# A graph network on one core: gathered rows come by node, are added in pairs on VectorE, and two one-hot products take the rest

## The chip, the cores and the metric

The kernel runs on one core of a Trainium2 chip. The core has a matrix engine (TensorE, PE in the profile, with its weight loads as PEld), VectorE (DVE), ScalarE (ACT), GpSimd (POOL) and the queue engine SyncE (SP); 16 DMA engines move data. The metric is device time in microseconds of one execution, the median of several runs.

## The reference

There are 6250 nodes with 256 float32 channels and 100,000 edges, sorted by destination. Four layers follow each other; each adds to every node the sum over its incoming edges and puts the result through three dense layers (64 channels in the middle of the last one).

```python
def agg(h):
    return jax.ops.segment_sum(h[src], dst, num_segments=N)
for l in range(NL - 1):                      # NL = 4
    h = x + agg(x)
    h = relu(h @ W1s[l] + b1s[l])
    h = relu(h @ W2s[l] + b2s[l])
    x = h @ W3s[l] + b3s[l]
h = x + agg(x)
h = relu(h @ cW1 + cb1); h = relu(h @ cW2 + cb2)
return h @ cW3 + cb3
# around it: x + ref(relu(layernorm(x)), src, dst, ...)
```

## The kernel before

The nodes form 49 blocks of 128. Since aggregation is linear, W1 is applied before it, and W3 of a layer is merged with W1 of the next. The current rows lie in `XY` in SBUF, as a high and a low half (float32r, 256 columns each), and in a table in HBM. The sums of a destination block are made in one of two ways.

**Panel products (L1470 to L1509).** For most blocks a matrix of edge counts (49 source blocks by 128 destinations, one byte each) is built once, in layer 0. Four blocks make a panel. For each of the 49 source blocks ("units"), a tile of counts is cast to float32r (L1464 on ACT, L1466 on DVE, some units ahead: `prepare`) and four products accumulate (two channel halves, high and low). The loop over layers, panels and units is the backbone of the order: `tick` counts units in `now`.

**Gathered blocks (class `Gathered`, L1264 to L1409).** For the other blocks the source rows are fetched by index: each indirect DMA on GpSimd's queue (L1309) brings 128 rows of 1 KB. The edges are packed in order of destination. Each half block (64 nodes) has 9 tiles of 128 edges, so a block has 18. VectorE makes one-hot matrices of 32 columns (L1334), and PE multiplies them with the rows in four column groups at once (L1353). A block takes two such "visits". Then VectorE adds the block's own row and the sums (L1371, L1380), PE transposes (L1391), and the dense layers follow (`mlp`: L1183, L1212).

In layer 0, 22 blocks are gathered, and 27 stand in seven panels, the first of which has three blocks. In layers 1 to 3, 18 blocks are gathered, and 31 stand in eight panels.

**The building of the matrices (`build`, L1013).** Of a block, 16 steps each make one-hots on VectorE (L994, one of each kind for two steps), multiply them on PE (L1035, two products a step) and cast the result to bytes (L1043 on ACT, L1045 on DVE, by turns). The steps of the first panel run ahead of the first product, all with their cast on ACT (`PRE` units); the others run beside the products of layer 0, by a list of goals.

**Pacing.** A planner's clock adds up the time that PE's work is expected to take (`passed`; the constants stand at L1420). `work_of(l)` is a layer's expected time. `Gathered.begin` spreads a layer's gathers evenly from the layer's start to 10 us before its end. Each row is asked for `LEAD` = 21 us ahead of the visits' schedule, and each gather also waits for the panel product that was last issued when it was asked for (`after`). `gath` has 24 row buffers in layer 0 and 26 later. Jobs such as transposes and dense layers have a first and a last unit, and run at a visit if one falls between.

**Preparation (`look`, L607; `normed`, L819).** The layer norm and the first product with W1 run for all nodes, and beside them the edge windows are found and fetched (`asks`, L601). For the gathered blocks, the tables of source indices (`idx`) and relative destinations (`rel`) are made here (L697 to L731 and L787 to L806). If a check finds that a half block has over 1152 edges, or another bound is passed, a general kernel (`any_edges`) runs afterwards.

Of the kernel before, what the change touches and what calls it, by code (L numbers as in the profile page):

```python
# [8 lines left out]
F32 = mybir.dt.float32  # L9
I32 = mybir.dt.int32  # L10
# [386 lines left out]
def sorted_edges(  # L397
# [56 lines left out]
    Q = P // 4  # L454
    TS = 9
    T = 2 * TS
    CUT = (3, 5)

    ROUNDS = [(3, 3), (4, 4), (0, 5), (1, 6), (2, 7), (None, 8)]
# [10 lines left out]
    gone = [(0, 4), (4, 4), (8, 4), (12, 4), (16, 1), (44, 4), (48, 1)]  # L470
    panels = [(17, 3), (20, 4), (24, 4), (28, 4), (32, 4), (36, 4), (40, 4), (44, 4)]
    S0 = 2 * panels[0][0]
    assert gone[-2] == panels[-1] and sorted(
        b + i for b, n in gone[:-2] + gone[-1:] + panels for i in range(n)) == list(range(NT))
    NQ = len(gone)
    PW = 4 * T

    left = [T * sum(n for _, n in gone[:q]) for q in range(NQ + 1)]

# [7 lines left out]
    clT = const.tile([P, 2, GSUB, NSUB - S0], BF16, name="clT")  # L487
    cT, loT = clT[:, 0], clT[:, 1]
    idx = const.tile([P, left[NQ]], I32, name="idx")
    rel = const.tile([P, left[NQ]], F32, name="rel")  # L490
# [7 lines left out]
    tables = [dram.tile([N, C], F32, name=f"table{l}") for l in range(NLAYER + 1)]  # L498
# [108 lines left out]
    def look(pool):  # L607
# [23 lines left out]
        nc.vector.memset(one, 1.0)  # L631
        firsts = pool.tile([1, EB], F32, name="near", bufs=1)
# [24 lines left out]

        place_i = pool.tile([P, NQ, PW], I32, name="hi", bufs=1)
        for q, (b, _) in enumerate(gone):
            nc.gpsimd.iota(place_i[:, q, :], pattern=[[1, PW]], base=T * b, channel_multiplier=-TS)  # L660
        place = pool.tile([P, 1], F32, name="place", bufs=1)
        nc.gpsimd.iota(place, pattern=[[0, 1]], base=0, channel_multiplier=P,
                       allow_small_or_imprecise_dtypes=True)
        node = pool.tile([P, GSUB], F32, name="node", bufs=1)
# [26 lines left out]
        for q in range(GSUB):  # L691
            for w, e in ((wd, dst), (ws, src)):
# [4 lines left out]
        both = pool.tile([P, 2], F32, name="both", bufs=1)  # L697
        sel = pool.tile([P, NQ, PW], F32, name="near_i", bufs=1)
        some = pool.tile([P, NQ, PW], F32, name="rel", bufs=1)
        nc.vector.tensor_copy(both[:NSUB, 0:1], first[:NSUB, 0:1])  # L700
        nc.vector.tensor_copy(both[:NSUB, 1:2], low[:NSUB])
        nc.vector.tensor_scalar(some[:NSUB], place_i[:NSUB], float(TS - 1), None, op0=OP.is_le)
        nc.vector.scalar_tensor_tensor(sel[:NSUB], place_i[:NSUB], 0.0, some[:NSUB],
                                       op0=OP.is_ge, op1=OP.mult)
        ps = ps_m.tile([P, W], F32, name="ps")
        for q in range(NQ):
            nc.tensor.matmul(ps[:PW, 2 * q:2 * q + 2], sel[:NSUB, q, :], both[:NSUB, :],
                             start=True, stop=True)
        spread = pool.tile([P, NQ, 2], F32, name="spread", bufs=1)
        nc.vector.tensor_copy(spread[:PW], ps[:PW, :2 * NQ].rearrange("p (q t) -> p q t", t=2))  # L710

        part = pool.tile([P, NQ], F32, name="part", bufs=1)
        nc.vector.scalar_tensor_tensor(part[:PW], spread[:PW, :, 1], float(-T), spread[:PW, :, 0],
                                       op0=OP.mult, op1=OP.add)
        for q, (b, _) in enumerate(gone):
            nc.vector.tensor_scalar(part[:PW, q:q + 1], part[:PW, q:q + 1], place[:PW, 0:1],
                                    float(T * P * b), op0=OP.add, op1=OP.add)
        skip = pool.tile([P, NQ], F32, name="skip", bufs=1)  # L720
        nc.vector.tensor_scalar(skip[:PW], part[:PW], float(E - P), None, op0=OP.min)
        from_i = pool.tile([P, NQ], I32, name="from_i", bufs=1)
        nc.vector.tensor_copy(from_i[:PW], skip[:PW])
        nc.vector.tensor_tensor(skip[:PW], part[:PW], skip[:PW], OP.subtract)
        base = pool.tile([P, NQ], F32, name="base", bufs=1)
        nc.vector.tensor_scalar(base[:PW], spread[:PW, :, 1], -1.0, None, op0=OP.add)
        gds = pool.tile([P, 2, NQ, P], I32, name="near_i", bufs=1)
        gd, gs = gds[:, 0], gds[:, 1]
        for q, (_, n) in enumerate(gone):
            for w, e in ((gd, dst), (gs, src)):  # L730
                asks.append((w[:n * T, q, :], e, from_i[:n * T, q:q + 1]))  # L731
# [3 lines left out]
        H = GSUB // 4  # L735
        for q0 in range(0, GSUB, H):
            cut = slice(q0, q0 + H)
            ask(len(asks) - 2 * (GSUB - q0 - H) - 2 * NQ)
            r = pool.tile([P, H, P], F32, name="rel", bufs=1)
            f = pool.tile([P, H, P], F32, name="f", bufs=1)  # L740
# [183 lines left out]
    with tc.manual_schedule():  # L924
# [163 lines left out]
        def job(first, last, fn):  # L1088

            jobs.append((now[0] + first, now[0] + last, fn))  # L1090

        queue = []

        def step(visit):

# [524 lines left out]
```

## Time and profile before

| | |
|---|---|
| median of 3 runs | 2350.51 us (2348.21 to 2352.5) |
| the profiled execution | 2343.82 us, span 2342.0 us |
| mean granted clock of PE | 0.98 |
| share of the span busy | PE 93%, DVE 42%, ACT 38%, POOL 61% |
| gathers | 1368 (396 in layer 0, 324 in each later layer) |
| panel products | 6076, of which 784 are 384 columns wide and 5292 are 512 wide |
| records of the one-hot products | 3344 (two to each of 1672 products) |
| HBM read and written | 310.61 and 58.07 MB |

Lines such as L1309 are those of the kernel before. A busy time is the time in which at least one instruction of a group ran. Matmuls overlap in their pipeline and their ends are modelled, so the time that one takes from PE is read from start to start, and a busy PE is not one at its peak.

### The profile page before, as it was taken

The numbers are of one execution on the slowest core, as the hardware profiler recorded it, in microseconds if no ns is written. First come the engines' busy times: TensorE is split into PE (matmuls) and PEld (weight loads), VectorE is DVE, ScalarE is ACT, GpSimd is POOL, SyncE is SP. The second block draws the span as 40 slices with busy tenths as digits, with TensorE's granted clock in tenths as the row PEclk, the third lists the DMA queues.
The fourth block names the chain that finished last, engine by engine and source line by source line (L and its number), as shares of the span: only waits on it lengthen the run. The fifth ranks groups of instructions, "written<-read, shape, count | busy, mean of one in ns | idle before, by whom it ended". The sixth has DMA issues, their size and how long they took to land. (4 is left out here: it accounts for less than half of the span.)

```text
span 2342.0 us, 34300 instructions
## 1 busy us (share of the span) xinstructions
PE 2175.8 (93%) x12062; PEld 1570.0 (67%) x12062; DVE 972.8 (42%) x2844; ACT 891.8 (38%) x1816; POOL 1429.4 (61%) x1442
## 2 busy tenths in 40 slices
PE   5888998999998999999999999999999999999898
PEld 3656666666665877676766877777677866666565
DVE  6887656556555422222223422222224423232222
ACT  4775545454545423232223432232233322222221
POOL 3635666666666266666666366666664566666663
PEclk9979999999999999999999999999999999999999
DMA  4545555555556554444455554545445655545553
GB/s 151 152 154 176 173 158 174 159 166 173 164 173 200 165 151 151 149 131 149 148 156 178 181 152 134 170 136 161 140 152 159 182 167 156 168 143 172 158 153 107
DMA packets 195882, 371.43 MB, mean 159 GB/s; under 512 B 32790, under 2 KB 122986, under 8 KB 195700
## 3 DMA queue, kind: packets, MB, share of 16 engines
q0 software_dynamic: 67264, 181.96, 26.9%
q1 hardware_dynamic: 126510, 185.34, 24.2%
q8 instruction: 96, 1.57, 0.3%
q10 hardware_dynamic: 1926, 1.85, 0.3%
q14 instruction: 86, 0.70, 0.1%
HBM read 310.61 MB, written 58.07 MB: 157 GB/s over the span
## 5 line engine op out<-in xcount | busy, mean ns | idle before, releaser
L1309 POOL DMA_INDIRECT rows<-table,idx x1368 | 1374.1, 1004 | 830.7 <-PE agg L1491 276.0
L1491 PE MATMUL agg<-a,XY 128*128 128x512 f32 (+1 forms) x6076 | 1484.3, 394 | 52.6 <-issue 39.0
L1491 PEld LDWEIGHTS agg<-a,XY 128*128 128x128 f32 x6076 | 1108.4, 189 | 334.6 <-issue 126.0
L1464 ACT CAST a<-at 128x512 fp32r<-128x512 uint8 (+1 forms) x943 | 546.9, 607 | 694.7 <-PE agg L1491 528.9
L1466 DVE CAST a<-at 128x512 fp32r<-128x512 uint8 (+1 forms) x576 | 256.2, 459 | 582.2 <-PE agg L1491 397.8
L1353 PE MATMUL sums<-rows,hot 128*32 128x256 f32 x3344 | 240.4, 387 | 8.1 <-issue 4.4
L1043 ACT CAST at<-bp 128x392 uint8<-128x392 f32 x276 | 131.3, 488 | 277.8 <-PE bp L1035 197.4
L1045 DVE CAST at<-bp 128x392 uint8<-128x392 f32 x220 | 124.1, 564 | 218.2 <-PE bp L1035 152.3
L1353 PEld LDWEIGHTS sums<-rows,hot 128*32 128x32 f32 x3344 | 106.0, 110 | 132.1 <-issue 72.2
L1035 PE MATMUL bp<-hi,lo 128*128 128x196 bf16 x992 | 143.7, 264 | 47.3 <-issue 18.7
L1035 PEld LDWEIGHTS <-lo 128*128 128x128 bf16 x992 | 76.0, 102 | 129.4 <-issue 86.6
L1380 DVE TENSOR_TENSOR u<-u,sums 128x256 f32<-128x256 f32 x76 | 31.8, 419 | 309.4 <-PE agg L1491 301.4
L1183 PE MATMUL ps<-h,w 128*128 128x512 f32 (+5 forms) x392 | 158.3, 544 | 0.5 <-issue 0.5
L994 DVE TENSOR_TENSOR hi<-cols,pairs 128x784 bf16<-128x784 bf16 x248 | 139.3, 562 | 0.0
L1212 PE MATMUL ps<-w,h 128*128 128x256 f32 x588 | 134.8, 380 | 3.4 <-PE ps L1212 1.6
L1334 DVE TENSOR_TENSOR hot<-colf,rel 128x64 f32<-128x64 f32 x836 | 126.9, 220 | 0.0
L1212 PEld LDWEIGHTS ps<-w,h 128*128 128x128 f32 x588 | 110.5, 190 | 20.2 <-issue 2.7
L1183 PEld LDWEIGHTS ps<-h,w 128*128 128x128 f32 (+1 forms) x392 | 67.2, 184 | 65.3 <-issue 56.4
L1230 DVE TENSOR_TENSOR zz<-ps,w 128x512 f32<-128x512 f32 (+1 forms) x78 | 50.2, 658 | 137.8 <-PE ps L1212 82.3
L994 DVE TENSOR_TENSOR lo<-lanes,pairs 128x512 bf16<-128x512 bf16 x248 | 104.2, 420 | 2.6 <-ACT pairs L989 1.4
L1186 ACT ACTIVATE h<-ps,bias 128x512 f32<-128x512 f32 (+5 forms) x98 | 60.6, 634 | 114.1 <-PE ps L1183 81.6
L1398 ACT ACTIVATE h<-ps,bias 128x256 f32<-128x256 f32 (+1 forms) x84 | 33.5, 450 | 149.4 <-PE agg L1491 48.8
(138 smaller groups left out, 744.9 us busy)
## 6 DMA issues: line engine op xcount, KB each, us to landing
at<-mat SPq DMA_DIRECT2D x189, 448.0 KB
mat<-at SPq DMA_DIRECT2D x31, 784.0 KB
rows<-table,idx POOLq DMA_INDIRECT x1368
table<-zz SPq DMA_DIRECT2D x69, 256.0 KB
back<-table SPq DMA_DIRECT2D x118, 128.0 KB
at<-mat SPq DMA_DIRECT2D x25, 336.0 KB
xs<-in_x_dram SPq DMA_DIRECT2D x8, 768.0 KB
table<-zs SPq DMA_DIRECT2D x24, 256.0 KB
```

Source lines behind the costliest of these rows:

```text
L994: nc.vector.tensor_tensor(o.rearrange("p q (n t) -> p q n t", t=2), values.rearrange("p (n t) -> p n t", t=2)[:, None, :, :].to_broadcast( ...
L1035: mm = nc.tensor.matmul(bp[:, m * HW:(m + 1) * HW], lo[:, q + m, :], hi[:, q + m, :], start=True, stop=True)
L1043: nc.scalar.copy(o, v)
L1045: nc.vector.tensor_copy(o, v)
L1183: mm = nc.tensor.matmul(ps[:mp, :w], weights[l][0][:, c, i * P:i * P + mp], h1[:, c, :w], start=(c == 0), stop=(c == KC - 1))
L1212: mm = nc.tensor.matmul(o, h2[0][:, c, nodes], w3[:, c, :], start=(c == 0), stop=(c == KC - 1))
L1309: got = nc.gpsimd.indirect_dma_start(out=t, out_offset=None, in_=tables[self.l][:, :], in_offset=bass.IndirectOffsetOnAxis(ap=idx[:, o:o + ...
L1334: nc.vector.tensor_tensor(hot[:, i, :, :], colf[:, None, i * Q:(i + 1) * Q].to_broadcast([P, 2, Q]), rel[:, o + k:o + k + TS + 1:TS, None] ...
L1353: nc.tensor.matmul(self.sums[(2 * h + m) * Q:(2 * h + m + 1) * Q, :C], self.hots[r, m][:, h, :], self.rows[g, h, k], start=(r == 0), stop= ...
L1464: nc.scalar.copy(o, mat[l, p][j])
L1466: nc.vector.tensor_copy(o, mat[l, p][j])
L1491: mm = nc.tensor.matmul(agg[c][:, :w], XY[:, j, o:o + P], a[:, :w], start=(j == 0 and half == 0), stop=(j == NT - 1 and half == 1))
```

## The change

The rows of a gathered block now come by node: gather k (k from 0 to 16) brings, for each of the 128 nodes, the row of its k-th edge. A node with fewer edges gets row N + p, one of 128 rows of zeros that are added to each table. Gathers 0 to 15 land in pairs, in 512-column tiles, and VectorE adds them: seven 128x512 adds. It then folds the two halves, gather 16 and the block's own row together (four 128x256 operations). What a node has beyond 17 edges goes to up to 256 overflow slots of its block, as two more gathers (`over`) and two one-hot products 128x128 by 128x256 on PE. A block thus has 19 gathers, and PE's sums are one visit.

Block 16 moves from the gathered blocks to the first panel, which now has four blocks: 21 blocks are gathered in layer 0 and 17 later, and 28 and 32 stand in panels. `PRE` follows, with 16 more build steps ahead of the first product.

In preparation each node's first edge and number of edges are found by counting (`count`), and the first 17 sources of each node are fetched by 21 indirect DMAs. The index table is finished at build step 50 (`slot_rows`), where layer 0's gathers now begin. The overflow slots of a block are found two blocks ahead (`overflow`: two products with two columns each, three small operations and one 256-wide one on VectorE, two indirect DMAs of one element to a partition). The bound of the check is now 256 overflow edges to a block.

Three in four of the byte casts beside the products now run on ACT (half before). The rows are asked for 13.0 us ahead in layer 0 and 16.5 us later (21 before). There are 7 pair buffers in layer 0 and 10 later, and four single ones; the build's PSUM pool has two buffers (three before), and the second cast ring 8 (9 before).

```diff
-    gone = [(0, 4), (4, 4), (8, 4), (12, 4), (16, 1), (44, 4), (48, 1)]
-    panels = [(17, 3), (20, 4), (24, 4), (28, 4), (32, 4), (36, 4), (40, 4), (44, 4)]
+    K, OV = 17, 2
+    SLOT = K + OV
+    gone = [(0, 4), (4, 4), (8, 4), (12, 4), (44, 4), (48, 1)]
+    panels = [(16, 4), (20, 4), (24, 4), (28, 4), (32, 4), (36, 4), (40, 4), (44, 4)]
...
+        zeros = pool.tile([P, C], F32, name="zeros", bufs=1)
+        for t in tables:
+            nc.gpsimd.dma_start(out=t[N:, :], in_=zeros)
...
+        def count(q0):
+            for t in range(1, GD):
+                nc.vector.tensor_scalar(below[:, t - 1], cT[:, q0:q0 + H, :], float(STEP * t),
+                                        None, op0=OP.is_lt)
...
+        for c in range(NG):
+            asks.append((idx[:, c, :], src, from_i[:, c:c + 1]))
...
+    def slot_rows():
+        nc.vector.scalar_tensor_tensor(live, idx, pad[:, 1:2], live, op0=OP.add, op1=OP.mult)
+        nc.vector.tensor_scalar(idx, live, pad[:, 0:1], None, op0=OP.add)
+
+    def overflow(hots, c):
+        nc.vector.tensor_scalar(hit, slots, gained[:, c:c + 1], None, op0=OP.is_ge)
+        for j in range(OV):
+            nc.tensor.matmul(ps[:, 2 * j:2 * j + 2], hit[:, j * P:(j + 1) * P], taken[:, c, :],
+                             start=True, stop=True)
+        def edges():
+            nc.vector.tensor_copy(rel[:, c, :], v[:, :, 0])
+            nc.vector.scalar_tensor_tensor(e, v[:, :, 1], nodes3[:, 2, c:c + 1], line, op0=OP.add,
+                                           op1=OP.add)
+            nc.vector.tensor_scalar(e_i, e, float(E - 1), None, op0=OP.min)
+        def gather():
+            for j in range(OV):
+                asks.append((over[:, j, c:c + 1], src, e_i[:, j:j + 1]))
+            ask(OV)
...
-                    if step % 2 or step <= 2 * PRE:
+                    if step % 4 != 2 or step <= 2 * PRE:
                         nc.scalar.copy(o, v)
                     else:
                         nc.vector.tensor_copy(o, v)
...
+                for g in range(len(self.blocks)):
+                    behind = 3 if g < len(self.blocks) - 1 else 0
+                    self.events.append((SLOT * g + 8, lambda g=g: self.spots(g), False))
+                    for k in range(3, K - 1, 2):
+                        self.events.append((SLOT * g + k, lambda g=g, k=k: self.pair(g, k), False))
+                    self.events.append((SLOT * g + K - 1, lambda g=g: self.fold(g), False))
+                    self.events.append((SLOT * g + SLOT - 1 + behind, lambda g=g: self.add(g), True))
...
-                for r in rounds:
-                    for h in range(2):
-                        for m, k in enumerate(ROUNDS[r]):
-                            if k is not None:
-                                nc.tensor.matmul(
-                                    self.sums[(2 * h + m) * Q:(2 * h + m + 1) * Q, :C],
-                                    self.hots[r, m][:, h, :], self.rows[g, h, k], start=(r == 0),
...
+            def pair(self, g, k):
+                t = self.rows.pop((g, k))
+                if k == 3:
+                    self.acc = work.tile([P, 2, C], F32, name="acc", bufs=1)
+                    nc.vector.tensor_tensor(self.acc, self.rows.pop((g, 1)), t, OP.add)
+                else:
+                    nc.vector.tensor_tensor(self.acc, self.acc, t, OP.add)
+
+            def spots(self, g):
+                hot = self.hot[g] = work.tile([P, OV, P], F32, name="hot", bufs=2)
+                nc.vector.tensor_tensor(hot, colf[:, None, :].to_broadcast([P, OV, P]),
+                                        rel[:, c, :, None].to_broadcast([P, OV, P]), OP.is_equal)
+
+            def fold(self, g):
...
+                nc.vector.tensor_tensor(u, u, self.acc[:, 0, :], OP.add)
+                nc.vector.tensor_tensor(u, u, self.acc[:, 1, :], OP.add)
+                nc.vector.tensor_tensor(u, u, self.rows.pop((g, K - 1)), OP.add)
+            def add(self, g):
+                for j in range(OV):
+                    mm = nc.tensor.matmul(sums[:, :C], hot[:, j, :], self.rows.pop((g, K + j)),
+                                          start=(j == 0), stop=(j == OV - 1))
...
-        LEAD, TAIL = 21.0, 10.0
+        TAIL = 10.0
+        LEADS, DEEP = (13.0,) + (16.5,) * NLAYER, (7,) + (10,) * NLAYER
...
-        ) as ps_a, tc.tile_pool(name="ps_b", bufs=3, space=PSUM) as ps_b:
+        ) as ps_a, tc.tile_pool(name="ps_b", bufs=2, space=PSUM) as ps_b:
+            READY = 50
+                if built[0] == READY:
+                    slot_rows()
+                    layers[0].begin()
```

More of the change, by code (lines that the diff above doesn't have):

```diff
@@ L705, in look @@
[L705 to L716, printed above, removed]
@@ L1117, in tick @@
                 first, last, fn = task
-                if first <= now[0] and (visit or last <= now[0]):
+                if max(first, held[0]) <= now[0] and (visit or last <= now[0]):
                     jobs.remove(task)
```

337 lines of the change are left out of this document (185 added, 152 removed).

## The prediction

> **What bounds the kernel now.** I read the profile page first, then the busy time of each engine by stage. The stages run from one change in the panel products to the next: preparation, the first panel's matrix, then the four layers.
>
> ```profile
> PE 2175.8 (93%) x12062; PEld 1570.0 (67%) x12062; DVE 972.8 (42%) x2844; ACT 891.8 (38%) x1816; POOL 1429.4 (61%) x1442
> ```
>
> ```profile
> 0.00:127.70 127.70, 91.20 (x418) 68.98 (x418) 95.18 (x257) 75.02 (x160) 55.26 (x74) 0.95 0.48 148
> 127.70:158.20 30.50, 22.77 (x114) 12.07 (x114) 26.77 (x63) 25.40 (x66) 9.20 (x8) 0.55 0.52 163
> 158.20:779.70 621.50, 567.20 (x3537) 389.66 (x3537) 370.87 (x1017) 319.40 (x703) 401.98 (x388) 0.99 0.54 167
> 779.70:1298.20 518.50, 504.14 (x2712) 375.74 (x2713) 159.93 (x504) 165.04 (x314) 320.68 (x324) 1.00 0.51 156
> 1298.20:1813.20 515.00, 502.05 (x2706) 374.87 (x2705) 155.80 (x499) 162.47 (x309) 320.54 (x324) 1.00 0.51 155
> 1813.20:2342.00 528.80, 488.49 (x2581) 348.67 (x2579) 164.26 (x507) 144.48 (x268) 321.71 (x324) 0.97 0.51 156
> ```
>
> The columns after the length are PE, PEld, DVE, ACT and POOL (busy us and count), granted clock, DMA. In layers 1 and 2 PE is busy 97% of the time at full clock and DVE 31%: a microsecond taken from PE there is a microsecond of the run. In layer 0 PE is busy 91%, DVE 60%, ACT 51%. PE hardly ever waits for gathered rows:
>
> ```profile
> PE bp L1035 <- ACT at L1043: 9.3, 12, 1.7
> PE agg L1491 <- ACT h L1507: 8.5, 5, 3.1
> PE bp L1035 <- DVE at L1045: 4.7, 3, 2.2
> PE bp L1035 <- DVE hi L994: 4.3, 7, 1.5
> PE bp L1035 <- DVE lo L994: 2.4, 2, 1.3
> PE sums L1353 <- DMA rows<-table,idx: 2.3, 4, 0.7
> ```
>
> These are PE's waits in layer 0 (us in all, times, longest). POOL looks free at 61%, but its own timeline says otherwise. In the middle of a layer, gathers stand back to back, and 0.30 us passes between two even when nothing is waited for:
>
> ```profile
> 448.95 0.96 POOL L1309 DMA_INDIRECT rows<-table,idx  x1 [0.30 <-issue]
> 450.21 0.95 POOL L1309 DMA_INDIRECT rows<-table,idx  x1 [0.30 <-issue]
> ```
>
> So a gather costs POOL its own time and 0.30 us. In layer 0 that is 401.98/388 = 1.036 + 0.30 = 1.34 us, in layers 1 to 3 about 320.7/324 = 0.990 + 0.30 = 1.29 us. The gathers of layer 0 run from the first of these rows to the second, those of layer 1 from the third to the last:
>
> ```profile
> 159.49 0.95 POOL L1309 DMA_INDIRECT rows<-table,idx  x1 [19.10 <-PE agg L1491]
> ...
> 759.48 0.95 POOL L1309 DMA_INDIRECT rows<-table,idx  x1 [0.30 <-issue]
> 798.93 1.19 POOL L1309 DMA_INDIRECT rows<-table,idx  x1 [38.50 <-ACT a L1464]
> ...
> 1282.22 0.96 POOL L1309 DMA_INDIRECT rows<-table,idx  x1 [0.30 <-issue]
> ```
>
> That is 600/388 = 1.55 us a gather in layer 0 and 483/324 = 1.49 in layer 1: POOL is at 87% of what it can issue in both. PE binds, and POOL is close behind.
>
> **The change part by part.** PE's prices come from its timeline in layer 2 (start, length, count of matmul records). A float32 product is two records; a panel product is one.
>
> ```profile
> 1358.81 2.75 PE L1212 MATMUL ps<-w,h 128*128 128x256 f32 x12
> 1361.49 1.50 PE L1353 MATMUL sums<-rows,hot 128*32 128x256 f32 x24
> 1362.92 10.27 PE L1491 MATMUL agg<-a,XY 128*128 128x512 f32 x44
> ...
> 1310.05 21.85 PE L1491 MATMUL agg<-a,XY 128*128 128x384 f32 x124
> ```
>
> *One-hot products.* A visit takes 1362.92 - 1361.49 = 1.43 us, and there are two to a block. The new two products have the form of the first row: 2.68/12 = 0.223 us a record, four records, 0.89 us a block. The wider first panel: 10.27/44 - 21.85/124 = 0.057 us on each of 196 products, 11.2 us a layer.
>
> Layers 1 to 3, each: -36 x 1.43 + 17 x 0.89 + 11.2 = -25.2 us; one block fewer to transpose gives 0.3 more. Three layers: **-76 us**, all on the path, if POOL and DVE keep up.
>
> Layer 0: -44 x 1.43 + 21 x 0.89 + 11.2 = -33.0 us on PE. The overflow step adds two 2-column products to a block. No row has that form; between 0 and 0.3 us each, I take 0.13, 5 us for the 19 blocks that fall in the layer: -28 us.
>
> *A fourth block ahead of the first product.* 16 more build steps run in the second stage, where PE's granted clock is 0.55:
>
> ```profile
> 140.11 5.42 PE L1035 MATMUL bp<-hi,lo 128*128 128x196 bf16 x24 [0.18 <-ACT at L1043]
> 146.39 1.65 PE L1035 MATMUL bp<-hi,lo 128*128 128x196 bf16 x8 [0.86 <-DVE hi L994]
> 148.22 0.83 PE L1035 MATMUL bp<-hi,lo 128*128 128x196 bf16 x4 [0.18 <-ACT at L1043]
> ```
>
> 32 records, or 16 steps, take 148.22 - 140.11 = 8.1 us: **+8 us**. DVE is nearly full there (26.77 of 30.50), so the two passes that finish the index table and the overflow steps of two blocks come on top, about +3 us. In preparation, four counting passes, the node tables and 21 index fetches take the place of seven blocks' edge tables; DVE's work there is about equal, between 0 and +6 us; I take +2. Four stores of zero rows join POOL's queue in that stage, where POOL is busy 55 of 128 us: nothing.
>
> *VectorE.* Prices (mean ns behind the busy time), as this view groups them:
>
> ```profile
> L994 DVE TENSOR_TENSOR hi<-cols,pairs 128x784 bf16<-128x784 bf16 x248 | 139.3, 562 | 0.0
> L1334 DVE TENSOR_TENSOR hot<-colf,rel 128x64 f32<-128x64 f32 x836 | 126.9, 220 | 0.0
> L1045 DVE CAST at<-bp 128x392 uint8<-128x392 f32 x220 | 124.1, 564 | 218.2 <-PE bp L1035 152.3 <-PE agg L1491 49.9 <-remote 14.9
> ...
> L1371 DVE TENSOR_TENSOR u<-XY 128x256 f32<-128x256 f32 x76 | 31.8, 419 | 0.0
> ...
> L1202 DVE TENSOR_TENSOR xt<-xt,cb3r 128x512 f32<-128x512 f32 x21 | 13.6, 685 | 0.0
> ```
>
> A pair add has the form of L1202, 685 ns; seven to a block. Three more 256-wide adds and a 256-wide one-hot go by L1371, 419 ns. A block gains 7 x 0.685 + 4 x 0.419 = 6.5 us and loses 126.9/76 = 1.7. Layers 1 to 3 gain 17 x 6.5 - 18 x 1.7 = 80 us each on a DVE with 360 us idle: hidden, at nothing. What hides it is the idle time and the five or six panel tiles that are cast ahead; if an add waited for late rows, the casts queued behind it on DVE would be late, and PE after them. Layer 0 gains 99 us, plus some 17 for the overflow step, and loses 110 casts of 564 ns (62 us): about 425 of 621 us. ACT takes those 110 casts: +54 us, 373 of 621. Neither engine is full, but in every second pair both casts now go to ACT and the products have two PSUM buffers, not three. The waits for casts and one-hots quoted above sum to 20.7 us; they may double or, with PE held elsewhere, vanish; I take +4.
>
> *GpSimd.* Layer 0 still has 399 gathers (396 before), and 38 overflow fetches come into it. Such a fetch has this row's form, about 1.07 + 0.30 us:
>
> ```profile
> L601 POOL DMA_INDIRECT ws<-in_src_dram,starts x16 | 17.0, 1060 | 4.9 <-issue 4.9
> ```
>
> And a gather that begins while a two-input SBUF operation runs on DVE takes longer:
>
> ```profile
> 137.66 0.56 DVE L994 TENSOR_TENSOR hi<-cols,pairs 128x784 bf16<-128x784 bf16 x1
> 137.81 1.23 POOL L1309 DMA_INDIRECT rows<-table,idx  x1 [0.30 <-issue]
> ...
> 139.15 0.42 DVE L994 TENSOR_TENSOR lo<-lanes,pairs 128x512 bf16<-128x512 bf16 x1
> 139.34 1.05 POOL L1309 DMA_INDIRECT rows<-table,idx  x1 [0.30 <-issue]
> ```
>
> The first began with 0.41 us of DVE's operation left and lost 0.28 against 0.95; the second with 0.23 left lost 0.10. So the loss is what is left, less 0.13. A pair add of 0.685 us catches a gather's start in 0.55/1.4 = 40% of cases and costs it 0.28 on average: 0.11 us; a 0.419 one costs 0.03. A block of 19 gathers gains (7 x 0.11 + 5 x 0.03)/19 = **0.05 us a gather**. Bounds: 0 if the adds always fall between starts, and 0.36 if every microsecond of these adds (6.9 a block) delayed POOL in full. I take 0.05.
>
> The Trainium skill (SBUF — State Buffer, § Who interferes with whom) says that a DVE instruction with two SBUF inputs contends with a GpSimd instruction that reads SBUF, and that whoever issues first holds the shared pair for the whole instruction. The two rows agree in kind and come 0.13 us cheaper than a full hold; by the rule to the letter layer 0 would lose some 12 us more than by the rows.
>
> POOL in layer 0 then needs 395 x (1.34 + 0.05) + 38 x 1.37 = 601 us after the first product, which starts at 158.2 + 8 + 3 + 2 = 171. (Pacing lets only four of the 399 go earlier; before, eight went.) The last gather goes out at 772; with 3 us to land and some 12 of work behind it the layer ends at 787, and at 791 with the cast waits. By PE alone it would end at 779.7 - 28 + 13 = 765. **POOL ends last in layer 0**: rows come late, DVE waits for them in order, PE waits for DVE. Against 779.7 this is **+11 us**, where PE's list promised -15.
>
> In layers 1 to 3 POOL needs 323 x (1.29 + 0.05) = 433 us. The window shrinks from 483 by 25, and by 5 more as the last row is asked for earlier ahead of its use: 453. At 96% it holds, with a few late rows: **+5 us** for the three.
>
> Sum: -76 + 11 + 5 = **-60 us**. The profiled execution took 2343.8 us (span 2342.0 and 1.8 around it), 6.7 below the median of 2350.5. Forecast 2283.8 for such an execution, **2290 us** as a median; its own range, from the bounds of the gather's delay (0 to 0.09) and the cast waits, 2272 to 2312.
>
> **The rivals.**
>
> *PE binds everywhere.* If the adds fall between gather starts and POOL catches up during PE's long float32 stretches, layer 0 ends near 765: -76 - 15 = -91, **2259 us**. For it: POOL had 13% slack. Against it: the 38 fetches and PE's shorter list use up the slack by themselves. Chance 0.20.
>
> *POOL binds in layers 1 to 3 too.* At 0.10 us a gather the need is 323 x 1.39 = 449 of 453, and any unevenness is lost; layer 0 ends near 811. -76 + 31 + 20 = -25: **2325 us**. Chance 0.15.
>
> *Slower: the adds hold up the gathers.* The price is the delay of a gather, e. Layer 0 grows by 4 us for each 0.01 of e, the later layers by 3.2 each once 323 x (1.29 + e) exceeds 453, at e = 0.11. At e = 0.14 the gain is gone; at 0.20 layer 0 ends at about 850, and each later layer needs 481 + 41 = 522 against about 520. +71 and 3 x 2: **2427 us**. For it: adds run when rows land, that is while POOL issues. Against it: only a start is caught. Chance 0.16.
>
> *It doesn't do what it says.* If a block has over 256 edges beyond 17 a node, the general kernel runs afterwards, at a price far above all of these. The given edges have at most 191. Chance 0.01.
>
> **How the numbers follow.** Forecast 0.44 (2272 to 2312), with 0.04 left for something within 0.2% of 2350.5, about what a measurement here tells from no change. Faster: 0.44 + 0.20 + 0.15 = 0.79; same 0.04; slower 0.17. The range 2250 to 2370 leaves out the far end of the first rival (0.04) and most of the slower cases (0.13).
>
> **What would show it.** Right: the sums' matmuls fall to 288 records; in layers 1 to 3 PE stays at 96% or more and each is about 490 us long; in layer 0 POOL's gathers stand 0.30 us apart nearly throughout, and DVE waits for rows. The mean gather shows e: 1.00 us before, about 1.05 after. Wrong: layer 0 ends by 770 with gaps on POOL (first rival); layers 1 to 3 above 500 us with DVE waiting for rows (the others); PE waiting for casts in layer 0 by over 30 us, which I priced at 4.

## The result, and the profile after

The changed kernel takes **2439.68 us** (median of 4 runs, 2436.01 to 2444.74), the kernel before 2351.51 beside it (4 runs, 2348.21 to 2352.9): ratio 1.0379, interval 1.0356 to 1.0401. It is 3.8% slower; the forecast was 2290 and its range ended at 2370. The profiled execution has a span of 2438.2 us, 96.2 more than before. First the page's line of busy times, then the busy time by stage with the columns of the prediction. The stages are cut at the same events: preparation, the first panel's matrix, four layers.

```profile
PE 2121.0 (87%) x9071; PEld 1576.9 (65%) x9071; DVE 1243.0 (51%) x2785; ACT 960.3 (39%) x1925; POOL 1521.2 (62%) x1495
```

```profile
0.00:131.20 131.20, 91.02 (x445) 70.35 (x445) 92.97 (x258) 74.61 (x155) 47.11 (x68) 0.93 0.47 144
131.20:192.30 61.10, 31.83 (x151) 16.71 (x151) 38.41 (x96) 34.46 (x85) 25.72 (x26) 0.53 0.31 95
192.30:877.70 685.40, 561.82 (x2681) 403.46 (x2681) 419.95 (x969) 370.27 (x809) 452.13 (x433) 0.92 0.50 154
877.70:1394.50 516.80, 484.16 (x1970) 368.15 (x1971) 226.56 (x484) 165.61 (x305) 332.50 (x323) 0.99 0.51 157
1394.50:1910.70 516.20, 480.21 (x1971) 368.27 (x1971) 228.35 (x484) 164.63 (x305) 331.55 (x323) 0.99 0.51 156
1910.70:2438.20 527.50, 471.95 (x1857) 349.98 (x1855) 236.72 (x496) 150.73 (x270) 332.16 (x323) 0.95 0.51 158
```

PE has 55 us less to do, as most of the one-hot products are gone, and yet the run is longer. The first product comes 34 us later (192.3, was 158.2), layer 0 is 64 us longer, and layers 1 to 3, where 25 us each should have gone, are as long as before (518.5, 515.0 and 528.8). In layer 1 PE's busy time fell by 20 us (504.14 to 484.16) and its idle time rose by 18 (14.4 to 32.6).

PE's waits in layer 0, then one line of VectorE's waits there:

```profile
PE bp L1108 <- ACT at L1116: 47.7, 26, 8.4
PE bp L1108 <- issue: 43.5, 30, 4.4
PE bp L1108 <- DVE hi L1067: 7.6, 8, 2.8
PE bp L1108 <- DVE at L1118: 5.5, 5, 1.8
```

```profile
DVE acc L1420 <- DMA rows<-table,idx: 2.4, 1, 2.4
```

PE waits for the byte casts (47.7 us, 9.3 before) and, for another 43.5, for nothing that the profile shows. VectorE hardly waits for rows, and GpSimd needs only 452.13 + 433 x 0.30 = 582 of the 685 us. So the engine that was to end last in layer 0 does not: the forecast's mechanism is not what this profile shows.

**A hand-off in layer 1 shows what does hold engines up here.** This is its timeline: PE transposes two blocks (L1472), and ScalarE then takes them out (L1479). Only the rows of these two engines are shown.

```profile
1036.03 0.62 ACT L1545 CAST a<-at 128x512 fp32r<-128x512 uint8 x1 [0.92 <-PE agg L1572]
1036.13 0.60 PE L1472 MATMUL ps<-ident,u 128*128 128x128 f32 x4
1036.48 5.76 PE L1572 MATMUL agg<-a,XY 128*128 128x512 f32 x24
1043.19 0.84 ACT L1479 ACTIVATE h<-ps,bias 128x256 f32<-128x256 f32 x2 [6.55 <-issue]
1043.92 0.62 ACT L1545 CAST a<-at 128x512 fp32r<-128x512 uint8 x1
1044.59 0.73 PE L1572 MATMUL agg<-a,XY 128*128 128x512 f32 x2 [2.34 <-ACT h L1479]
```

The transposes end at 1036.73 and ScalarE is free from 1036.65, but it starts at 1043.19, 6.5 us later. Its casts stand behind, PE uses up the six tiles that are cast (24 products) and then stands still for 2.3 us. ScalarE waits for PE's semaphore alone there, so the signal reached it late. In the trace's records such signals are updates of semaphores. After one at 1040.31 the next of PE's is recorded at 1046.02, and six stand between 1046.02 and 1046.28: a pause and then a burst. ScalarE's start at 1043.19 has no update of its own on record. PE has 2825 instructions that raise its semaphore, and only 2477 separate updates are recorded (2685 and 2277 in the profile of before). Whether the others arrived together with one of these or are only missing from the records can't be told.

### The profile page after: what moved, and what is told of

It reads as the page before. It is cut to its first block, busy times and chain, and to the rows that moved or that the text cites. A ratio compares the mean times of both kernels' runs of the same rounds, so it can differ in the third digit from the quotient of the medians.

```text
span 2438.2 us, 28824 instructions
## 1 busy us (share of the span) xinstructions
PE 2121.0 (87%) x9071; PEld 1576.9 (65%) x9071; DVE 1243.0 (51%) x2785; ACT 960.3 (39%) x1925; POOL 1521.2 (62%) x1495
## 5 line engine op out<-in xcount | busy, mean ns | idle before, releaser
L1572 PE MATMUL agg<-a,XY 128*128 128x512 f32 x6076 | 1593.2, 412 | 85.1 <-issue 46.0
L1394 POOL DMA_INDIRECT rows<-table,idx x1152 | 1181.8, 1026 | 667.5 <-PE agg L1572 258.8
L1545 ACT CAST a<-at 128x512 fp32r<-128x512 uint8 x943 | 564.4, 622 | 801.1 <-PE agg L1572 527.1
L1547 DVE CAST a<-at 128x512 fp32r<-128x512 uint8 x576 | 256.6, 452 | 598.6 <-PE agg L1572 371.4
L1422 DVE TENSOR_TENSOR acc<-acc,rows 128x512 f32<-128x512 f32 x432 | 295.8, 685 | 2.5 <-DMA rows<-table,idx 0.4
L1394 POOL DMA_INDIRECT last<-table,over x144 | 155.4, 1079 | 58.9 <-issue 28.7
L1260 PE MATMUL ps<-h,w 128*128 128x512 f32 (+2 forms) x364 | 160.4, 576 | 13.9 <-DVE zz L1301 6.8
L1118 DVE CAST at<-bp 128x392 uint8<-128x392 f32 x110 | 62.0, 564 | 115.3 <-PE bp L1108 78.6
L1394 POOL DMA_INDIRECT last<-table,idx x72 | 77.6, 1078 | 30.7 <-issue 14.3
L1461 DVE TENSOR_TENSOR u<-u,sums 128x256 f32<-128x256 f32 x72 | 30.1, 418 | 99.5 <-PE agg L1572 94.7
L1451 PE MATMUL sums<-last,hot 128*128 128x256 f32 x288 | 76.8, 387 | 4.3 <-DMA last<-table,over 3.2
```

The lines of the kernel that those rows point to most:

```text
L1118: nc.vector.tensor_copy(o, v)
L1260: mm = nc.tensor.matmul(ps[:mp, :w], weights[l][0][:, c, i * P:i * P + mp], h1[:, c, :w], start=(c == 0), stop=(c == KC - 1))
L1394: got = nc.gpsimd.indirect_dma_start(out=t, out_offset=None, in_=tables[self.l][:, :], in_offset=bass.IndirectOffsetOnAxis(ap=at, axis=0),)
L1422: nc.vector.tensor_tensor(self.acc, self.acc, t, OP.add)
L1451: mm = nc.tensor.matmul(sums[:, :C], hot[:, j, :], self.rows.pop((g, K + j)), start=(j == 0), stop=(j == OV - 1))
L1545: nc.scalar.copy(o, mat[l, p][j])
```

## The experiments

Theories, as the expectations name them. **A**: too many byte casts on ScalarE, and too few PSUM buffers. **B**: the pair adds stand ahead of casts and one-hots in VectorE's queue. **C**: the second cast ring is a tile too short. **D**, formed after the first four runs: semaphore updates that come late in bursts hold up both kernels, the changed one more. **E**: without bursts GpSimd ends last in layer 0 of the changed kernel, which is the forecast's own mechanism, and in layer 3 as well. The experiments ran in five groups, each on a chip of its own, so each ratio is to the kernel before on the same chip.

### Casts, buffers and the ring

`half_casts` puts back one line, `three_buffers` one number (the overflow step then takes its PSUM from the same pool), `ring_nine` two:

```diff
-                    if step % 4 != 2 or step <= 2 * PRE:
+                    if step % 2 or step <= 2 * PRE:
...
-name="ps_b", bufs=2
+name="ps_b", bufs=3
...
-(7,) + (10,) * NLAYER
+(7,) + (9,) * NLAYER
-name="rings2", bufs=AHEAD + 5
+name="rings2", bufs=AHEAD + 6
```

> The changed kernel with one thing put back: half of the byte casts beside the products go to ScalarE, not three in four. Theory A (in layer 0 the products wait for casts because ScalarE has too many of them and the build has only two PSUM buffers): PE's waits for the cast on L1116 in layer 0 fall from 47.7 us to under 20 and layer 0 from 685 to about 655 us; layers 1 to 3 stay at 517, 516 and 528; total about 2410. Theory B (VectorE's pair adds stand ahead of casts and one-hots in its queue): VectorE now has 110 casts more, so layer 0 gets no shorter, 685 or more; total 2440 or more.

> The changed kernel with three PSUM buffers for the build (two before this edit); the overflow step takes its PSUM from the same three. Theory A: waits for casts in layer 0 fall by half or more, layer 0 about 650 us, and the first panel's building is 10 us shorter; total about 2395. Theory B: a third buffer lets one more step wait, layer 0 670 to 680; total about 2425. Both: layers 1 to 3 unchanged.

> The changed kernel with the second cast ring back at 9 tiles (8), paid for with one pair buffer (9 for 10) in layers 1 to 3. Theory C: the casts are ready 7 to 8 us ahead again, and each of the layers 1 to 3 falls by 15 to 20 us; total about 2385. Theory B: the casts still stand behind the adds in VectorE's queue, under 5 us a layer; total about 2430. Layer 0 unchanged by both.

Measured: 2203.89 us (ratio 1.0139, interval 1.0073 to 1.0205), 2199.28 (1.0118, 1.0079 to 1.0157) and 2202.14 (1.0131, 1.0068 to 1.0194). On this chip the kernel before takes 2174.96 us, 177 less than in the result above, which no expectation had foreseen. `after_third`, the changed kernel as it is on another such chip, has 1.0122 (below): none of the three differs from it. Only the first product comes earlier with three buffers, at 166.1 us against 171.3.

`both_back` has the first two edits together; `sizes_only` is the kernel before with the change's three sizes and nothing else.

> The changed kernel with half of the byte casts on ScalarE and three PSUM buffers, both at once. Theory A: what each alone does not give they give together, layer 0 falls by 20 us or more against the changed kernel run beside it. Otherwise within 8 us of it.

> The kernel before with the change's three sizes alone: three in four byte casts on ScalarE, two PSUM buffers for the build, 8 tiles in the second cast ring. Rows still come by edge and go through one-hot products. Theories A and C: 20 to 60 us slower than the kernel before. Theory B (the adds): within 8 us of it.

Measured on a chip with bursts: 2409.91 us (1.0395, 1.0363 to 1.0426) against 2404.38 for the changed kernel there, and 2317.78 (1.0002, 0.998 to 1.0025). Theory A falls on both kinds of chip: the sizes cost the kernel before nothing, and putting the casts and buffers back gives the changed kernel nothing. Theory C falls without bursts; with bursts only `sizes_only` speaks against it, as `ring_nine` did not run there.

### The two kernels unchanged, on other chips

> The kernel before, unchanged, for its profile on the chip of the other experiments, where it has taken 2175 us and not 2351. Theory D (on the first chip something outside the program held PE up in all four layers, and the changed kernel more than this one): its layers 1 and 2 are well under the 518.5 and 515.0 of the first profile, about 485 to 495, and the pitch of the panel products (start to start) exceeds 0.24 us by under 10 us in all a layer, not 20. If only layer 0 or preparation is shorter here, D falls.

> The changed kernel, unchanged, as the control for the four experiments run so far. If it takes about 2200 us on a chip where the kernel before takes 2175 (ratio 1.01), then putting back half of the casts (2204), the third buffer (2199) or the ninth ring tile (2202) each gave nothing, and theories A and C fall there; if it takes 2230 or more (ratio 1.025), each of the three gave some 30 us. Layers 1 to 3 by theory D: about 470 each. On the first chip again: 2440 us, ratio 1.038.

> The kernel before, unchanged, for its profile on the chip of this call. So far the time of this kernel went with the chip: 2351 and 2318 us on two, where the semaphore updates of PE, VectorE and ScalarE came late in bursts (in the profile of before on the second, PE's updates stood still for a mean of 2.5 us, 274 times), and 2175 on one where no profile of the changed kernel shows a burst. Theory D (late semaphore updates; before is held up less, as its casts lie further ahead): on a chip with bursts 2310 to 2355 us, layers 1 and 2 508 to 518 us; on one without bursts about 2175 us, and layers 1 and 2 at 485 to 495. If a profile without bursts takes over 2300 us, theory D falls.

> The changed kernel, unchanged, beside the other three. Theory D: ratio 1.035 to 1.042 on a chip with bursts; on one without bursts ratio 1.010 to 1.015, layers 1 to 3 at 470, 469 and 479 (some 20 us each less than before's on that chip, the gain that was forecast), and layer 0 longer by 25 to 35 us than before's.

On the second chip, with bursts: before 2318.47 us, the changed kernel 2404.38, ratio 1.039 (1.0345 to 1.0434). `before_again` was expected to show layers of 485 to 495 us; on this chip, which has bursts too, layers 1 and 2 take 514 and 508. On a chip without bursts: 2177.02 and 2205.64, ratio 1.0122 (1.0074 to 1.017). The busy time by stage of the kernel before there, and of the changed one:

```profile
148.00:707.10 559.10, 551.46 (x3536) 384.92 (x3536) 370.20 (x1017) 323.07 (x703) 408.32 (x388) 1.00 0.59 186
707.10:1203.20 496.10, 495.17 (x2712) 375.23 (x2713) 165.62 (x504) 166.99 (x314) 316.32 (x324) 1.00 0.52 163
1203.20:1697.10 493.90, 493.90 (x2708) 374.09 (x2706) 163.43 (x499) 165.36 (x309) 316.38 (x324) 1.00 0.52 162
1697.10:2171.70 474.60, 466.02 (x2581) 345.98 (x2579) 169.50 (x507) 147.74 (x268) 319.21 (x324) 0.99 0.55 174
```

```profile
171.30:785.10 613.80, 540.64 (x2681) 387.60 (x2681) 416.17 (x969) 370.20 (x809) 457.64 (x433) 0.96 0.55 172
785.10:1254.60 469.50, 465.18 (x1971) 368.26 (x1972) 229.20 (x484) 168.94 (x305) 329.83 (x323) 1.00 0.56 173
1254.60:1724.40 469.80, 466.45 (x1971) 368.93 (x1970) 229.99 (x484) 168.73 (x305) 330.49 (x323) 0.99 0.55 172
1724.40:2201.80 477.40, 447.64 (x1857) 341.35 (x1855) 234.32 (x496) 153.88 (x270) 326.78 (x323) 0.98 0.55 175
```

What the change does to each stage, in us of the profiled executions:

| | first product | layer 0 | layer 1 | layer 2 | layer 3 | sum |
|---|---|---|---|---|---|---|
| forecast | +13 | -2 | -24 | -24 | -23 | -60 |
| without bursts | +23.3 | +54.7 | -26.6 | -24.1 | +2.8 | +30.1 |
| first chip, with bursts | +34.1 | +63.9 | -1.7 | +1.2 | -1.3 | +96.2 |
| second chip, with bursts | +26.9 | +54.2 | -3.5 | +2.6 | +2.9 | +83.1 |

(The forecast's -76 and +5 are shared out over layers 1 to 3.) The same hand-off as above, on the chip without bursts:

```profile
1351.63 0.60 PE L1472 MATMUL ps<-ident,u 128*128 128x128 f32 x4
...
1352.26 0.84 ACT L1479 ACTIVATE h<-ps,bias 128x256 f32<-128x256 f32 x2 [2.52 <-PE ps L1472]
```

ScalarE starts 0.03 us after the transposes end. From the moment at which the transposes have ended and ScalarE is free, the start comes after 0.04 us on average without bursts (42 hand-offs of the kernel before, 38 of the changed one). On the first chip it comes after 1.4 us on average in the kernel before (longest 7.3) and 1.9 in the changed one (longest 7.9). Without bursts 2684 separate updates are recorded for the 2685 instructions of the kernel before that raise PE's semaphore. The Trainium skill (Perfetto Trace Analysis, § Tensor Engine Instruction) has an update pushed when the results are written and then spread to all engines, outside the time that the profile gives the instruction. In these hand-offs 0.04 us lie between the end and the next start in one place and up to 7.9 in the other; which part of that is the spreading isn't shown. Why there are bursts, no run here shows. Each chip was used at one time only, so whether they belong to the chip or to the time isn't known either, nor whether the first chip is one of the five.

So the loss has two parts. Some 30 us are there without bursts. The other 53 and 66 come with bursts, most of them as the missing gain of layers 1 and 2 (23 to 27 us each).

### The adds on VectorE

```diff
-                    nc.vector.tensor_tensor(self.acc, self.acc, t, OP.add)
+                    nc.vector.tensor_tensor(self.acc[:, :, :8], self.acc[:, :, :8], t[:, :, :8], OP.add)
```

> The changed kernel with six of the seven pair adds of a block narrowed from 2x256 to 2x8 columns; it leaves out most of those sums, and keeps every gather and every wait for rows. VectorE loses about 6 x 0.6 = 3.6 us a block. Theory B: layers 1 to 3 fall by about 20 us each, to 497, 496 and 508, and layer 0 by 30 or more, total about 2350. Theory A and theory C (the second cast ring, which is one tile shorter, makes the casts late in layers 1 to 3): layers 1 to 3 change by under 5 us each, layer 0 by under 10; total 2420 to 2440.

> The changed kernel with six of the seven pair adds of a block narrowed to 2x8 columns, as in narrow_adds (it leaves out most of those sums), now beside the unchanged kernel. Theory B: 80 us or more below the changed kernel, most of the loss. Theory D: the waits on late updates stay; 25 to 45 us below the changed kernel, some 7 to 10 us in each of the layers 1 to 3 and the rest in layer 0, whichever chip it is.

> The changed kernel with six of the seven pair adds of a block narrowed to 2x8 columns (most of those sums are left out), on the chip of this call. On two chips without bursts it gained 35 to 39 us. On a chip with bursts: theory B (casts stand behind adds on VectorE) says layers 1 to 3 fall by 15 us or more each, ratio to before under 1.01; theory D says 3 to 8 us each, ratio 1.018 to 1.03, since the adds themselves are no handoff of PE's.

Measured on three chips, none with bursts: 2166.35 (0.9957, 0.9943 to 0.9971), 2170.64 (0.9968, 0.9952 to 0.9983) and 2168.22 us (0.9968, 0.9953 to 0.9984). That is about 35 us below the changed kernel, and not theory B's 80. Beside `after_third`, layer 0 falls by 22.4 us in `narrow_adds2`, layers 1 to 3 by 6 to 7 each (in the other two runs layer 0 is 18 and 20 us shorter than in `after_third`, and layer 3 some 3). Layer 0 of `narrow_adds2`:

```profile
172.00:763.40 591.40, 533.75 (x2681) 386.40 (x2681) 354.00 (x969) 368.79 (x809) 434.34 (x433) 0.96 0.57 179
```

GpSimd's busy time in layer 0 falls by 457.64 - 434.34 = 23.3 us, about as much as the layer: 23.3/433 = 0.054 us a gather (0.043 and 0.049 in the other two). As GpSimd's chain of gathers sets layer 0 without bursts (`sixteen`, below), the gathers that the adds hold up are enough to account for the fall. The edit relieves VectorE's queue too, and a share of its own wasn't separated. On a chip with bursts this wasn't tried.

### A longer lead for the casts

```diff
-(7,) + (10,) * NLAYER
+(7,) + (7,) * NLAYER
-                prepare(u + 1 + (AHEAD if l == 0 else AHEAD + 2))
+                prepare(u + 1 + (AHEAD if l == 0 else AHEAD + 4))
-name="rings2", bufs=AHEAD + 5
+name="rings2", bufs=AHEAD + 8
```

> The changed kernel with a longer lead of the casts in layers 1 to 3: the second ring has 11 tiles (8), tiles are cast 7 units ahead (5), and 7 pair buffers remain (10). Theory D: on a chip with bursts the waits for casts shrink, and layers 1 to 3 fall by 8 to 15 us each, ratio about 1.025; on a chip without bursts nothing is gained, within 8 us of the changed kernel, or 10 to 20 us lost if rows come late with three pair buffers fewer. Theory B (load on VectorE): nothing gained on either.

> The changed kernel with 11 tiles in the second cast ring (8), tiles cast 7 units ahead (5) and 7 pair buffers (10), on the chip of this call. Without bursts it gave nothing (2202 against 2206). On a chip with bursts: theory D says layers 1 to 3 fall by 8 to 15 us each as fewer late updates reach PE, ratio about 1.025; if they fall by under 4 us, the shorter lead of the casts is not how the bursts reach PE.

Both runs fell on chips without bursts: 2202.13 us (1.0106, 1.0062 to 1.015) and 2197.24 (1.0103, 1.0063 to 1.0143), the same as the changed kernel within the noise. What they were meant to tell under bursts stays open.

### GpSimd's work

`sixteen` gathers 16 rows by node (the fetches of overflow edges just hold the rest), so a block has 18 gathers; `no_overflow` drops the calls that find and fetch overflow edges and sets their tables to constants.

```diff
-    K, OV = 17, 2
+    K, OV = 16, 2
...
-                    for k in range(3, K - 1, 2):
+                    for k in range(3, K, 2):
...
-                    if k < K - 1:
+                    if k < K:
...
-                nc.vector.tensor_tensor(u, u, self.rows.pop((g, K - 1)), OP.add)
```

> The changed kernel with 16 gathers by node and not 17 (the overflow of the gathered blocks then has at most 254 edges, still within two fetches): 18 gathers a block, eight pairs and no single row, one 256-wide add less and one pair add more. GpSimd's work falls by 21 gathers in layer 0 (21 x 1.36 = 28 us) and 17 in each later layer (22 us). Theory E (without bursts GpSimd ends last in layers 0 and 3): on a chip without bursts layer 0 falls by 20 to 28 us and layer 3 by 10 to 18, layers 1 and 2 by under 5, total about 2165 against 2205. On a chip with bursts theory D says that GpSimd does not bind and the handoffs stay as many: 5 to 15 us in all.

> The changed kernel without the finding of the overflow edges: it leaves out what a node has beyond 17 edges, reads rows of zeros for those two gathers of each block and multiplies them by an empty one-hot. Gathers and products stay as many; 42 fetches of GpSimd (38 in layer 0), 42 small products and 84 small operations of VectorE and 42 one-hots of 256 go. Theory E: on a chip without bursts layer 0 falls by 40 to 52 us (38 x 1.36 = 52 us of GpSimd), near before's 559; layers 1 to 3 stay. Theory D on a chip with bursts: each block's overflow step is a chain of handoffs (VectorE, PE, VectorE, GpSimd, VectorE), layer 0 falls by 10 to 30 us there, and most of its excess of 54 to 64 us stays.

Measured without bursts: 2152.35 us (0.9897, 0.9857 to 0.9937) and 2153.59 (0.9889, 0.9854 to 0.9924). `sixteen` by stage, from layer 0 on, to be read beside `after_third`, which ran on another such chip:

```profile
170.70:757.00 586.30, 532.26 (x2680) 384.87 (x2680) 407.70 (x948) 368.18 (x809) 435.54 (x412) 0.97 0.56 176
757.00:1225.80 468.80, 468.78 (x1970) 367.08 (x1971) 222.46 (x468) 168.86 (x305) 308.61 (x306) 1.00 0.54 168
1225.80:1694.50 468.70, 468.70 (x1971) 367.01 (x1970) 223.44 (x467) 168.63 (x305) 308.10 (x306) 1.00 0.53 168
1694.50:2150.00 455.50, 445.75 (x1857) 338.41 (x1855) 234.32 (x479) 153.82 (x270) 310.77 (x306) 0.99 0.56 178
```

Twenty-one gathers at 1.36 us are 28 us, and layer 0 falls by 27.5; seventeen at 1.31 are 22, and layer 3 falls by 21.9; layers 1 and 2 hardly change, as PE fills them (468.78 of 468.80). VectorE's waits for rows in layer 3 tell the same, first in `after_third`, then in `sixteen`:

```profile
DVE acc L1422 <- DMA rows<-table,idx: 87.5, 60, 4.7
DVE acc L1420 <- DMA rows<-table,idx: 72.6, 13, 8.6
```

```profile
DVE acc L1422 <- DMA rows<-table,idx: 11.0, 11, 3.4
```

`no_overflow` takes 41 us from layer 0 (613.8 to 572.5) and nothing from layer 3 (478.4 against 477.4), where it takes nothing from GpSimd:

```profile
171.30:743.80 572.50, 524.30 (x2642) 381.86 (x2642) 405.13 (x894) 368.39 (x809) 428.63 (x395) 0.97 0.59 185
1680.30:2158.70 478.40, 446.58 (x1857) 340.28 (x1855) 233.29 (x496) 153.78 (x270) 327.11 (x323) 0.98 0.55 174
```

Theory E is shown for chips without bursts.

> The changed kernel with 16 gathers by node, as in sixteen, timed in three rounds. On a chip without bursts: ratio 0.990, about 2152 us. On a chip with bursts: theory D (late updates bind, GpSimd has idle time) says it gains 5 to 15 us on the changed kernel, ratio 1.032 to 1.037; if GpSimd bound there too, layer 0 falls by 28 and layer 3 by 22, ratio about 1.018.

> sixteen with the longer lead of the casts in layers 1 to 3 (11 ring tiles, cast 7 units ahead, 7 pair buffers). On a chip without bursts: within 8 us of sixteen, 2145 to 2160 us. On a chip with bursts, theory D with the short lead as the way by which bursts reach PE: layers 1 to 3 fall by 8 to 15 us each against sixteen, 25 to 45 us in all; under 12 us in all, the lead of the casts is not the way.

Again without bursts: 2153.22 us (0.9906, 0.9889 to 0.9922) and 2150.66 (0.9889, 0.9872 to 0.9905). Both are some 1% faster than the kernel before there, and the longer lead is again worth nothing that shows. How `sixteen` does with bursts wasn't seen.

## Why the prediction was wrong

On the chip of the result two terms carry the miss: the -76 of layers 1 to 3 came out at -1.8, and the end of layer 0, forecast 11 us later, came 98.0 later (779.7 to 877.7).

- **"Layers 1 to 3: -76, all on the path, if POOL and DVE keep up."** The price was right: -26.6 and -24.1 us in layers 1 and 2 without bursts, forecast -25.2. The words "on the path" failed in two ways. On the first chip, PE's 97% busy time in layers 1 and 2 of before was read as "PE binds"; it held 9 us of products stretched by late signals (504.14 busy, 495.17 without bursts), and 13 more idle. There the changed kernel's idle time takes the whole gain back. Without bursts GpSimd did keep up in layers 1 and 2, with nothing to spare: in layer 1 its gathers stand 0.30 us apart throughout (21.4 to the first, 427.9 of gathers and 20.2 to the end are the 469.5), and PE fills 465.18 of it.
- **Layer 3** gains nothing anywhere. Without bursts PE's busy time there did fall by 18.4 us (466.02 to 447.64), but its idle time rose by 21 (8.6 to 29.8): the words "on the path" failed because GpSimd had no room left. These are its first and last gathers in the kernel before:

```profile
1713.00 0.95 POOL L1309 DMA_INDIRECT rows<-table,idx  x1 [33.66 <-DMA cw<-in_L_gnn_cW_dram]
...
2139.14 0.95 POOL L1309 DMA_INDIRECT rows<-table,idx  x1 [0.30 <-issue]
```

  Start 15.9 us into the layer, 427.1 us of gathers, and 31.6 to the end are its 474.6. The gathers and their gaps of 0.30 make 324 x (0.985 + 0.30) = 416 of the 427.1, so GpSimd was within 11 us of its limit. PE was full there too, and its waits are short and none is for rows, so GpSimd alone did not set the length:

```profile
PE ps L1209 <- ACT h L1186: 1.6, 2, 0.8
PE agg L1491 <- ACT a L1464: 0.3, 1, 0.3
```

  The change shortens PE's work and takes one gather of 324 away. In the changed kernel the three parts are 20.1, 424.9 and 32.5, the gathers 0.30 apart throughout, and fewer gathers shorten the layer (`sixteen`). I took layer 1's window of 453 us for all three layers; layer 3 has less work for PE (466.02 busy, 495.17 in layer 1), and without bursts its gathers had 427.1. The rival "POOL binds in layers 1 to 3 too" holds there in kind, at 1.31 us a gather and not its 1.39.
- **"POOL ends last in layer 0, which ends at 787."** Without bursts it ends at 785.1: GpSimd needs (457.64/433 + 0.30) = 1.357 us a gather (forecast 1.34 + 0.05), they stand 0.30 apart, VectorE waits for them, and PE for VectorE's one-hots:

```profile
DVE acc L1422 <- DMA rows<-table,idx: 80.1, 46, 5.9
PE bp L1108 <- DVE hi L1067: 43.8, 39, 5.0
```

  That the end itself agrees is partly luck: the gathers need 433 x 1.357 = 588 us, forecast 601, and 21 us follow the last one, forecast 15. And what it costs hangs on where the layer ended before: 707.1 there, not the 779.7 of the first profile, 72 us of which came with the bursts. So +11 became +78. On the first chip the mechanism fails: the layer ends at 877.7 with GpSimd idle for 100 us.
- **"Cast waits +4"** is the term that failed on the first chip. PE's waits for casts and one-hots in layer 0 sum to 60.8 us (47.7 + 7.6 + 5.5), where 20.7 were quoted before, and the waits for nothing that shows to 43.5, where they were 18.3. The forecast had named over 30 us of waiting for casts as a sign against it. Fewer casts on ScalarE and a third buffer do not change the time on the second chip with bursts (`both_back`), so the late signal is the likelier cause; that it is the only one was not shown.
- **First product +13** came out at +23 without bursts and +34 on the first chip. Without bursts the steady building starts at 128.5, not 120.1 (8 us, forecast 2), and 32 records, or 16 steps, take 9.0 us, not 8.1. Here are the ends of such a stretch, first of the kernel before, then of the changed one:

```profile
129.89 5.43 PE L1035 MATMUL bp<-hi,lo 128*128 128x196 bf16 x24 [0.18 <-DVE hi L994]
136.17 1.65 PE L1035 MATMUL bp<-hi,lo 128*128 128x196 bf16 x8 [0.85 <-DVE hi L994]
138.00 5.42 PE L1035 MATMUL bp<-hi,lo 128*128 128x196 bf16 x24 [0.18 <-DVE hi L994]
```

```profile
138.46 0.83 PE L1108 MATMUL bp<-hi,lo 128*128 128x196 bf16 x4 [0.66 <-DVE hi L1067]
139.54 0.87 PE L1108 MATMUL bp<-hi,lo 128*128 128x196 bf16 x4 [0.25 <-ACT at L1116]
140.60 0.87 PE L1108 MATMUL bp<-hi,lo 128*128 128x196 bf16 x4 [0.19 <-ACT at L1116]
...
147.44 0.83 PE L1108 MATMUL bp<-hi,lo 128*128 128x196 bf16 x4 [0.67 <-DVE hi L1067]
```

  With two buffers PE stops 0.19 us for a cast every other step, all through the stage, of which I priced nothing; with three the first product comes 5 us earlier. The 16 added steps cost 9 us, forecast 8.
- **e, the delay of a gather by the adds**, was right over the whole run and not by layer. Narrowing 432 adds took 48.8 us from GpSimd in `narrow_adds2`, 0.11 us an add, as forecast; but it is 0.054 us a gather in layer 0 and 0.021 to 0.029 in the later ones, forecast 0.05 everywhere. And e was added to a mean that already held the delays by VectorE's work of before, of which one-hots and casts went: without bursts the whole gather grew only from 408.32/388 = 1.052 to 457.64/433 = 1.057 in layer 0, and from 316.32/324 = 0.976 to 329.83/323 = 1.021 in layer 1. That the work that went makes the difference wasn't tried. On the first chip the mean gather of rows went from 1004 to 1026 ns over the run:

```profile
L1394 POOL DMA_INDIRECT rows<-table,idx x1152 | 1181.8, 1026 | 667.5 <-PE agg L1572 258.8
L1422 DVE TENSOR_TENSOR acc<-acc,rows 128x512 f32<-128x512 f32 x432 | 295.8, 685 | 2.5 <-DMA rows<-table,idx 0.4
```

- **The adds "hidden, at nothing"** on VectorE was right, apart from e: their own price is the 685 ns forecast. Layers 1 to 3 shorten by 6 to 7 us each when they shrink (`narrow_adds2`), and so does GpSimd's chain of gathers (in layer 1 from 427.9 to 421.3 us).
- **The rival "Slower: the adds hold up the gathers"** gave the right sign for a wrong reason: it wanted e = 0.20.

What stays open is how the bursts reach PE more in the changed kernel. A cast began 8.6 us (median) ahead of its product in the later layers of the first profile of before, and 4.8 in that of the changed kernel, and a signal that is 6 us late outruns 4.8 us. That is an argument and was not shown: `long_ring` never met a burst, and `sizes_only`, whose lead is 7.7 us, lost nothing under them.

## What to carry to other kernels

A high busy share in a profile doesn't say that an engine binds: take a hand-off with nothing between its two instructions and read how long after the producer's end the consumer starts, before you price anything. Where an engine issues at a fixed gap (here 0.30 us between gathers), work out its whole stage, start lag + count x (mean + gap) + tail, for each stage by itself: it gave layer 0 and layer 3 of the changed kernel to within a few us, and there a gather less was worth 1.3 us. It fits layers 1 and 2 as well (21.4 + 427.9 + 20.2 = 469.5), where a gather less was worth nothing, since PE was as full: before you take work from one engine, see whether another is full beside it. Run both kernels on more than one chip before you trust a gain that hangs on tight timing.

## What the runs showed of the hardware

- The kernel before takes 2351 us on the first chip and 2318 on the second with bursts, and 2173 to 2177 us on four others, with the same median pitch of the panel products (0.227 us). All 6 profiles with 12 to 17% fewer updates of PE's semaphore on record than instructions that raise it are from the former. All 14 in which the two numbers agree to within 4 are from the latter.
- In those 6 profiles ScalarE starts 0.9 to 1.9 us on average after PE's transposes once nothing else holds it, and up to 8.7 us. In each of the 14 it is 0.04 us on average.
- Narrower adds on VectorE shorten gathers that GpSimd issues at the same time: 1025 to 996 ns on average with six of seven adds narrowed, between two kernels on one chip.
